# Reads, a short chain and the order of tasks in a fused attention and gated feed-forward layer

## The chip, the cores and the metric

The kernel runs on one core of a Trainium2 chip. The metric is the device time of one execution in microseconds; three runs of the kernel before have a median of 5631.06 us (5629.08 to 5638.95). Beside them there is one profiled execution, on which all readings below rest. Lines (L701) are lines of the kernel before; engines are named TensorE (PE, with its weight loads as PEld), VectorE (DVE), ScalarE (ACT), GpSimd (POOL) and SyncE (SP), which issues all DMAs here.

## What is computed

The input is `x` with 8 batches of 2048 tokens of 512 values. All is float32.

```python
xn = layernorm(x)
q, k, v = xn @ Wq.T + bq, xn @ Wk.T + bk, xn @ Wv.T + bv      # 8 heads: 8 wide for q and k, 64 for v
scores = einsum("bmhd,bnhd->bhmn", q, k) / sqrt(8)
scores = where(scores >= 0, scores, 0.2 * scores)
s = gamma * (softmax(scores) @ v) + xn
base = xn @ W.T
logits = l2norm(xn @ Wp.T + bp) @ l2norm(sim) * exp(min(temp, CLAMP))   # 4 experts
lw = softmax(logits)
ret = where(expert == argmax(lw), lw, 0)
res = sum over experts of ret * (xn @ Wd.T) @ Wu.T            # ranks 1, 2, 4, 8
out = x + s * silu(base + res)
```

## The kernel before

**Tiles and loops.** Tokens are cut into 4 blocks of 512 a batch, heads into 4 pairs. A *sequence step* `s` is one batch, one pair of heads and one block of queries; there are 8 x 16 = 128 of them, and each loops over 16 chunks of 128 keys (`i`). One pass of the inner loop is called a half step: 2048 in all. A half step does, in TensorE's order: the row shift onto the scores of chunk `i` for the first head (`less_max`, L657), the scores of the next chunk (`score`, L640), one unit of the maxima of a later sequence step (`max_unit`, L586), the row shift for the second head, and then either attention weights times values (`weigh`, L681) or a piece of background work. ScalarE makes the leaky slope (L651) and the exp (L669) of both heads; VectorE reduces the unit of maxima from PSUM (L597, into `mxr`); GpSimd adds the exp tile to a running sum (`add_up`, L701, 128 x 1024 float32).

**PSUM.** Scores have two pairs of banks, `mx` of the maxima has one buffer of two banks, `av` one, and all background work and the endings share one bank, `m`.

**Order.** The order of instructions on each engine is written out by hand, by three generators that the loop resumes: `queue[0]` an ending, `queue[1]` the shift rows, `queue[2]` the background tasks. What a generator yields says what may come next: IDLE (resume me once in the next half step, `go_on`), WAIT (nothing else of the background in between), TINY, HOLD, FREE, SLOW (TensorE pieces of several sizes, which `half_full` puts where weights times values would stand, or which `half_light` does in the last batch). `due_at` spreads the tasks' costs over time.

**Shift rows** (`shift_rows`, L597 to L631). At half step 6 of a sequence step the maxima of the next one are complete, and VectorE reduces `mxr` to `m` (L603). In the next half step it takes `big = 0.2 * min(m, 0)` (L609) and `m = max(m, 0)` (L610), and GpSimd does six operations of 128 x 8 (L611 to L616): the sum, and a split into a high and a low part by the factor -4097, into a tile `c`. Both engines work through their queues in order, so these six stand in front of the next L701. Two half steps later VectorE transposes `c` (L621), and eight small DMAs carry the rows through DRAM to `shift`.

**Background tasks.** `project_block` makes queries, keys and values of a block of the next batch (transposes L370 and their copies L373, projections L265 and L279). `lift_block` makes the gate and the feed-forward of a block: in its gate, the logits are multiplied into the bank `gps` (L446), and a chain of some 14 small VectorE operations (L456 to L479) and one exp (L460) turns them, in place in PSUM, to the chosen expert's weight, in three groups with a WAIT between them; copies spread the weight to `rx`. The tasks of a batch are written in the order lift 1, lift 2, project 0, project 1, lift 3, project 2, project 3. `norm` runs the layer norm's statistics of a block ahead of its `project_block`.

**Endings** (`ending`, L703). After the last weights times values of a sequence step: `av` is copied out (L708), three DMAs read rows of the lifted block (`gs` from GS, `xs` from the input and from XN, L714 to L717), after three more half steps TensorE sums `acc` over keys (L724) and transposes (L741), and VectorE divides (L732 to L743), adds XN (L744), multiplies by `gs` (L747) and adds the input (L748). The result goes out from `gs`.

**Start-up.** The first batch's projections and the gate's constants are made ahead of the loop (L863 and on). Two lines of it are spoken of below: L207 multiplies two small SBUF tiles into `simn`, and L222 subtracts two SBUF tiles of 32 x 512 into `wu_sb`; L434, in `lift_block`, is GpSimd's power of four elements a partition.

Of the kernel before, what the change touches and what calls it, by code (L numbers as in the profile page):

```python
# [8 lines left out]
FP = mybir.dt.float32  # L9
# [23 lines left out]
def fused_layer_kernel(  # L33
# [113 lines left out]

    hi_bits = filled("hi_bits", HI_BITS, I32)
    minus_one = filled("minus_one", -1.0)
    splitter = filled("splitter", -4097.0)  # L150
    ln_eps = filled("ln_eps", LN_EPS)

    kst = []
# [144 lines left out]
    def norm(b, n):  # L298
# [24 lines left out]
        normalize(0)  # L323
        normed[b, n] = xn, normalize

    def fetch(b, n):
        xnT = two.tile([128, NC, BLK], FP, name="xnT")
        nc.sync.dma_start(out=xnT, in_=XT[b][n])
        fetched[b, n] = xnT
# [31 lines left out]
    def project_block(b, n, prefetch):  # L361

        for _ in stats.pop((b, n)):
            pass
        xn, normalize = normed.pop((b, n))
        xnT = two.tile([128, NC, BLK], FP, name="xnT")
        for t in range(NT):
            tp = bank([128, NC, 128], "tp")
            for c in range(NC):
                nc.tensor.transpose(tp[:, c, :], xn[:, t, c * 128 : (c + 1) * 128], ident)  # L370
            if t + 1 < NT:
                normalize(t + 1)
            nc.vector.tensor_copy(xnT[:, :, t * 128 : (t + 1) * 128], tp)  # L373
            spend(0.5)
            yield TINY if t + 1 < NT else FREE
        if prefetch:
            fetch(*prefetch)
        nxt = b * NB + n + 2
        if nxt < B * NB:
            load_x(nxt // NB, nxt % NB)  # L380

        ps = bank([128, BLK], "qkps")
        yield from project(ps, wqk_sb, columns(xnT))
        nc.scalar.activation(ps, ps, AF.Identity, bias=bqk_sb)
        yield WAIT
        hi = one.tile([128, BLK], FP, name="hi")
        lo = one.tile([128, BLK], FP, name="lo")
        split_keys(b, n, ps, hi, lo)
        nc.sync.dma_start(out=XN[b][n], in_=xn)
        nc.sync.dma_start(out=XT[b][n], in_=xnT)  # L390
        if n == NB - 1:
            ready.append(b)
        yield FREE

        vb = one.tile([128, NPAIR, NT, 128], FP, name="vb")
        for t in range(NT):
            ps = bank([128, C], "vps")
            yield from token_major(ps, wv_sb, columns(xnT), t)
            add_bias(vb, t, ps)
            yield FREE if prefetch or t + 1 < NT else TINY  # L400
        store_values(b, n, vb)
        if n == NB - 1:
            valued.append(b)

    def lift_block(b, n, prefetch, cols=None):
# [35 lines left out]
        dn = one.tile([128, BLK], FP, name="dn")  # L441
        nc.scalar.copy(dn, ps)
        yield TINY
        gps = bank([128, NT, 2 * NEXP], "gps")
        for t in range(NT):
            nc.tensor.matmul(  # L446
                gps[:, t, 0:NEXP],
                lhsT=pw[:, t * 128 : (t + 1) * 128],
                rhs=simn,
                start=True,  # L450
                stop=True,
            )
        spend(1.0)
        shape = [128, NT, NEXP]
        lg = gps[:, :, 0:NEXP]
        nc.vector.tensor_tensor(lg, lg, nrm.to_broadcast(shape), ALU.mult)  # L456
        red = sm.tile([128, NT, 1], FP, name="red")
        nc.vector.reduce_max(red, lg, axis=AX.X)
        nc.vector.tensor_tensor(lg, lg, red.to_broadcast(shape), ALU.subtract)
        nc.scalar.activation(lg, lg, AF.Exp)  # L460
        yield WAIT
        nc.vector.reduce_sum(red, lg, axis=AX.X)
        nc.vector.reciprocal(red, red)
        nc.vector.tensor_tensor(lg, lg, red.to_broadcast(shape), ALU.mult)

        nc.vector.reduce_max(red, lg, axis=AX.X)
        pick = gps[:, :, NEXP : 2 * NEXP]
        nc.vector.tensor_tensor(pick, lg, red.to_broadcast(shape), ALU.is_equal)
        nc.vector.tensor_tensor(
            pick, pick, prio.unsqueeze(1).to_broadcast(shape), ALU.mult  # L470
        )
        yield WAIT
        nc.vector.reduce_max(red, pick, axis=AX.X)
        own = sm.tile(shape, FP, name="own")
        nc.vector.tensor_tensor(own, pick, red.to_broadcast(shape), ALU.is_equal)
# [123 lines left out]
    def shift_rows(s):  # L599
        if s >= B * SEQ:  # L600
            return
        m = sm.tile([128, 2 * NT, 1], FP, name="m")
        nc.vector.reduce_max(m, mxr.pop(s).rearrange("p e t n -> p (e t) n"), axis=AX.X)  # L603
        yield IDLE

        ml = sm.tile([128, 2 * NT], FP, name="ml")
        c = parts[s % 2][:, 0 : 4 * NT].rearrange("p (i m) -> p i m", i=2)
        big = sm.tile([128, 2 * NT], FP, name="big")
        nc.vector.tensor_scalar(big, m[:, :, 0], 0.0, SLOPE, ALU.min, ALU.mult)  # L609
        nc.vector.tensor_scalar_max(m[:, :, 0], m[:, :, 0], 0.0)  # L610
        nc.gpsimd.tensor_tensor(ml, m[:, :, 0], big, ALU.add)  # L611
        nc.gpsimd.tensor_tensor(big, ml, splitter.to_broadcast([128, 2 * NT]), ALU.mult)
        nc.gpsimd.tensor_tensor(ml, ml, minus_one.to_broadcast([128, 2 * NT]), ALU.mult)
        nc.gpsimd.tensor_tensor(c[:, 1, :], big, ml, ALU.subtract)
        nc.gpsimd.tensor_tensor(c[:, 0, :], big, c[:, 1, :], ALU.subtract)
        nc.gpsimd.tensor_tensor(c[:, 1, :], ml, c[:, 0, :], ALU.subtract)  # L616
        for _ in range(2):
            yield IDLE

        cT = sm.tile([128, 32], FP, name="cT")  # L620
        nc.vector.transpose(cT, parts[s % 2])  # L621
        for q in range(4):
            nc.sync.dma_start(
                out=SH[s % 2][:, :, :, q, :].rearrange("i e t j -> (i e t) j"),
                in_=cT[32 * q : 32 * q + 4 * NT, :],
            )
        shift = qp.tile([128, BLK], FR, name="shift")
        for g in range(4):
            nc.sync.dma_start(
                out=shift[STK * g : STK * g + 2, :].bitcast(FP),  # L630
                in_=SH[s % 2][:, g % 2].rearrange("i t q j -> i (t q j)"),  # L631
            )
        shifts[s] = shift
# [59 lines left out]
    def add_up(s, i, ex):  # L693
# [6 lines left out]
            acc[s] = two.tile([128, 2, BLK], FP, name="acc")  # L700
        nc.gpsimd.tensor_tensor(acc[s], old, ex, ALU.add)  # L701

    def ending(s):  # L703

        b, p, n = where(s)
# [2 lines left out]
        nc.vector.tensor_copy(avs, avt.pop(s))  # L708
        yield IDLE
        sums = acc.pop(s)  # L710
        while (b, n) not in lifted:
            yield IDLE
        gs = two.tile([128, NT, 128], FP, name="gs")
        nc.sync.dma_start(out=gs, in_=GS[b][n][:, :, cols])  # L714
        xs = two.tile([128, 2, NT, 128], FP, name="xs")
        nc.sync.dma_start(out=xs[:, 0], in_=xv[b, n][:, :, cols])
        nc.sync.dma_start(out=xs[:, 1], in_=XN[b][n][:, :, cols])  # L717
        for _ in range(3):
            yield IDLE
        yield TINY  # L720
# [34 lines left out]
    for b in range(B):  # L755
        order = [(lift_block, b, 1, A2), (lift_block, b, 2, A2)]
        if b + 1 < B:
            order += [(project_block, b + 1, 0, A1), (project_block, b + 1, 1, A1), (lift_block, b, 3, A2)]
            order += [(project_block, b + 1, 2, A1), (project_block, b + 1, 3, A1)]
        else:  # L760
            order += [(lift_block, b, 3, A2)]
        total = sum(o[3] for o in order) - (16 * MM if b + 1 < B else 0.0)
        t0, run = SEQ * b + LIFTED, 0.0
        for f, bb, n, cost in order:
            run += cost
            at = min(run / total, 1.0) * ((KEYED if b + 1 < B else LAST) - LIFTED) + t0
            if run > total + 0.01:
                tasks.append((f, bb, n, cost - 16 * MM, at))
                tasks.append((None, bb, n, 16 * MM, SEQ * b + VALUED))
            else:  # L770
                tasks.append((f, bb, n, cost, at))
        if b + 1 < B:
            tasks.append((lift_block, b + 1, 0, A2, SEQ * (b + 1) + LIFTED))
# [7 lines left out]

    def behind():
        jobs = [t for t in tasks if t[0]]
        for k, (f, b, n, _, _) in enumerate(jobs):
            g, bb, nn = (jobs[k + 1] if k + 1 < len(jobs) else (None, 0, 0))[:3]
            if g is project_block:
                stats[bb, nn] = norm(bb, nn)
            if k == 0:
                yield from opening
            else:  # L790
                yield from f(b, n, (bb, nn) if g is lift_block else None)

    back = behind()
    opening = iter(())
    holder = []
    queue = [None, None, back]
    state = [IDLE, IDLE, IDLE]
    due = [0]

    def go(j):  # L800
        state[j] = next(queue[j], None)
# [3 lines left out]

    def ahead():

        return holder or [k for k in (1, 0, 2) if queue[k] is not None and state[k] != IDLE]

    def go_on():  # L810

        for j in range(3):
            if queue[j] is not None and state[j] == IDLE:
                go(j)
        if holder and state[holder[0]] == WAIT:
            go(holder[0])
            return True
# [68 lines left out]
    with tc.manual_schedule():  # L886
# [143 lines left out]
        for s in range(B * SEQ):  # L1030
            for i in range(CH):
                if i <= 3 and s + 2 not in qst and (where(s + 2)[0] in (0, *ready) or i == 3):
                    load_stacks(s + 2)
                if i >= 6 and s + 1 not in vts and (where(s + 1)[0] in valued or i == 13):
                    load_values(s + 1)
                due[0] = due_at(s + (i + 1) / CH)
                u = s * CH + i + CH + LEAD
                nxt = s * CH + i + 1
# [66 lines left out]
```

## Time and profile before

| | us |
|---|---|
| median of three runs | 5631.06 |
| profiled execution | 5619.18 |
| its span | 5617.4 |
| TensorE busy in it | 5378.9 |
| GpSimd busy | 4779.1 |
| ScalarE busy | 4440.7 |
| VectorE busy | 3673.9 |
| mean granted TensorE clock (share of full) | 0.968 |

In the lists of groups a line gives the code line, engine and operation, what is written and read, the shape, the number of instructions, then their busy time and the mean duration of one in ns, then the idle time of the engine just before them and what ended most of it. In a list of waits the three numbers are the sum in us, how often, and the longest. A timeline gives start and length in us, then engine, line and operation; several like instructions in a row are merged (x3). In a table of windows the columns are the stretch, its length, the busy time of TensorE, its weight loads, VectorE, ScalarE and GpSimd (with counts), then the granted TensorE clock, the DMA share and GB/s.

### The profile page before, as it was taken

To read this page: it belongs to the slowest core of one execution; us is meant where nothing else is said; L and a number is where in the kernel's file an instruction comes from. 1 tells how busy PE (TensorE), PEld (TensorE's weight loads), DVE (VectorE), ACT (ScalarE), POOL (GpSimd) and SP (SyncE) were. 2 spreads that over 40 slices of the span, in tenths; PEclk is the share of its full clock that TensorE was granted. 3 is DMA by queue.
4 is the path that set the end of the run, shared out by engine and by line. 5 is a ranking of instruction groups with operands and counts; after the bars stand their busy time and mean duration, and the time that the engine had idled before them with its cause. 6 is when DMAs were issued, how large, how long until landed. Compare 5 with 4: busy or idle time off the path is not lost.

```text
span 5617.4 us, 78032 instructions
## 1 busy us (share of the span) xinstructions
PE 5378.9 (96%) x26258; PEld 1999.1 (36%) x26258; DVE 3673.9 (65%) x4988; ACT 4440.7 (79%) x8627; POOL 4779.1 (85%) x2906
## 2 busy tenths in 40 slices
PE   8999999999999999999999999999999999999998
PEld 3333333333333333333333333333333333333332
DVE  5577666766676666667666666666766766645653
ACT  2788878888888878888788887888878888767777
POOL 1789988888888888888888888888888888878878
PEclk9999999999999999999999999999999999979989
DMA  5333432434324343252432434234343333322221
GB/s 197 106 112 121 128 113 88 128 106 147 104 78 142 93 146 95 76 158 91 142 92 83 147 112 130 80 111 131 107 123 99 102 120 122 100 78 78 71 63 61
DMA packets 528264, 615.38 MB, mean 110 GB/s; under 512 B 44092, under 2 KB 438332, under 8 KB 491768
## 3 DMA queue, kind: packets, MB, share of 16 engines
q1 hardware_dynamic: 527864, 610.39, 35.6%
q8 instruction: 209, 3.42, 0.3%
q14 instruction: 191, 1.56, 0.1%
HBM read 407.88 MB, written 202.38 MB: 109 GB/s over the span
## 4 chain that ended last, share of the span: by engine, by line
PE 80%; ACT 8%; DVE 7%; DMA 2%; issue 2%; SPq 1%; POOL 1%; POOLq 0%; ACTq 0%; DVEq 0%
PE av L681 28%; PE sc L657 16%; PE zps L279 9%; PE vps L279 8%; PE mx L586 7%; ACT ex L669 5%; ACT sc L651 2%; PE pps L265 2%; DVE mxr L597 2%; PE qkps L265 2%; PE dps L265 2%; PE dps L724 1%; DMA xs<-XN 1%; PE atp L741 1%; DVE gs L748 1%
## 5 line engine op out<-in xcount | busy, mean ns | idle before, releaser
L701 POOL TENSOR_TENSOR acc<-acc,ex 128x1024 f32<-128x1024 f32 x1792 | 4231.0, 2361 | 301.7 <-ACT ex L669 189.3
L597 DVE TENSOR_REDUCE mxr<-mx 128x2 f32<-128x1024 f32 x2032 | 2480.2, 1221 | 1260.0 <-PE sc L657 1018.5
L669 ACT ACTIVATE ex<-sc 128x512 f32<-128x512 f32 x4096 | 2231.0, 597 | 972.2 <-PE sc L657 829.0
L651 ACT ACTIVATE sc<-sc 128x512 f32<-128x512 f32 x4096 | 2237.7, 593 | 18.9 <-PE sc L640 18.9
L681 PE MATMUL av<-ex,v_sb 128*64 128x512 f32 x8192 | 2149.5, 630 | 11.6 <-DVE avs L708 9.2
L657 PE MATMUL sc<-shift,ones_r 2*128 2x512 f32 x4096 | 1679.7, 463 | 75.5 <-ACT sc L651 66.9
L586 PE MATMUL mx<-k,q_sb 32*128 32x512 f32 x4096 | 1445.4, 454 | 37.0 <-DVE mxr L597 35.9
L657 PEld LDWEIGHTS sc<-shift,ones_r 2*128 2x128 f32 x4096 | 703.6, 187 | 1560.4 <-ACT sc L651 1450.5
L640 PE MATMUL sc<-q_sb,k 32*128 32x512 f32 x4096 | 1037.4, 503 | 0.0
L681 PEld LDWEIGHTS av<-ex,v_sb 128*64 128x64 f32 x8192 | 469.7, 138 | 839.6 <-issue 805.2
L586 PEld LDWEIGHTS mx<-k,q_sb 32*128 32x128 f32 x4096 | 562.2, 188 | 61.2 <-DVE mxr L597 49.4
L279 PE MATMUL zps<-w_sb,xnT 128*128 128x512 f32 (+1 forms) x1120 | 541.0, 597 | 32.7 <-DMA xnT<-XT 14.1
L279 PE MATMUL vps<-wv_sb,xnT 128*128 128x512 f32 x960 | 475.2, 619 | 7.4 <-DVE gs L748 7.2
L701 POOL TENSOR_TENSOR acc<-ex 128x1024 f32<-128x1024 f32 x128 | 301.8, 2358 | 197.3 <-ACT ex L669 197.3
L640 PEld LDWEIGHTS sc<-q_sb,k 32*128 32x128 f32 x4096 | 385.9, 185 | 0.8 <-issue 0.8
L279 PEld LDWEIGHTS zps<-w_sb,xnT 128*128 128x128 f32 x1120 | 187.6, 192 | 270.3 <-issue 247.9
L279 PEld LDWEIGHTS vps<-wv_sb,xnT 128*128 128x128 f32 x960 | 164.0, 189 | 209.7 <-issue 195.9
L518 DVE SCALAR_TENSOR_TENSOR g<-th,zps 128x512 f32<-128x512 f32 x128 | 88.0, 688 | 189.2 <-ACT th L517 189.2
L611 POOL TENSOR_TENSOR ml<-m,big 128x8 f32<-128x8 f32 x128 | 26.2, 205 | 176.6 <-DVE m L610 176.6
L349 DVE TENSOR_TENSOR vb<-vps,bv_sb 128x512 f32<-128x512 f32 x120 | 83.0, 691 | 95.6 <-PE vps L279 95.4
L265 PE MATMUL dps<-xnT,wd_sb 128*128 128x512 f32 (+1 forms) x280 | 139.1, 607 | 0.0
L265 PE MATMUL pps<-xnT,wp_sb 128*128 128x512 f32 (+1 forms) x280 | 130.9, 585 | 5.0 <-DVE gs L748 5.0
(124 smaller groups left out, 2656.7 us busy)
## 6 DMA issues: line engine op xcount, KB each, us to landing
v_sb<-VS SPq DMA_DIRECT2D x127, 1024.0 KB
k<-KS SPq DMA_DIRECT2D x256, 256.0 KB
XN<-xn SPq DMA_DIRECT2D x32, 1024.0 KB
q_sb<-QS SPq DMA_DIRECT2D x256, 128.0 KB
xnT<-XT SPq DMA_DIRECT2D x32, 1024.0 KB
GS<-g SPq DMA_DIRECT2D x32, 1024.0 KB
gs<-GS SPq DMA_DIRECT2D x128, 256.0 KB
xs<-in_x_dram SPq DMA_DIRECT2D x128, 256.0 KB
```

Source lines behind the costliest of these rows:

```text
L265: nc.tensor.matmul(ps[:, part], lhsT=wt[:, c, :], rhs=xnT[c][:, part], start=(c == 0 and part.start == 0), stop=(c == NC - 1 and part.stop ...
L279: nc.tensor.matmul(ps[:, part], lhsT=xnT[c][:, t * 128 : (t + 1) * 128], rhs=wt[:, c, part], start=(c == 0 and part.start == 0), stop=(c = ...
L349: nc.vector.tensor_tensor(vb[:, :, t, :], ps.rearrange("p (h d) -> p h d", h=NPAIR), bv_sb.rearrange("p (h d) -> p h d", h=NPAIR), ALU.add,)
L518: nc.vector.scalar_tensor_tensor(g[:, t, :], th, 1.0, ps, ALU.add, ALU.mult)
L586: nc.tensor.matmul(parts[e], lhsT=q_sb[r, t * 128 : (t + 1) * 128], rhs=k_sb[r, kb // 2 * BLK : (kb // 2 + 1) * BLK], start=True, stop=True,)
L597: nc.vector.reduce_max(mxr[s][:, :, t, kb : kb + 1], mx, axis=AX.X)
L640: nc.tensor.matmul(sc[e], lhsT=k_sb[r, i // 2 * 128 : (i // 2 + 1) * 128], rhs=q_sb[r, :], start=True, stop=True,)
L651: nc.scalar.activation(sc[e], sc[e], AF.Prelu, alpha=SLOPE)
L657: nc.tensor.matmul(sc[e], lhsT=ones_r[r, :], rhs=shifts[s][r, :], start=False, stop=True, skip_group_check=True,)
L669: nc.scalar.activation(ex[:, e, :], sc[e], AF.Exp, scale=qscale)
L681: nc.tensor.matmul(avt[s][64 * e : 64 * e + DV, :], lhsT=v_sb[:, i, 64 * e : 64 * e + DV], rhs=ex[:, e, :], start=(i == 0), stop=(i == CH ...
L701: nc.gpsimd.tensor_tensor(acc[s], old, ex, ALU.add)
```

## The change

Six edits, together:

- the endings' three reads are issued from the inner loop at chunk 12 and later of their own sequence step, if the block is lifted (`read_for_ending`); the ending itself only reads them where that has not happened;
- the six GpSimd operations and the two VectorE operations of the shift rows become four VectorE `scalar_tensor_tensor`, two in one half step and two in the next, the latter followed at once by the transpose; the loads of `shift` come one half step after it;
- the gate's chain works in the SBUF tiles `lg` and `pick` in place of the bank `gps`, and between its groups it yields TINY and resumes the next `project_block` once (its first two groups of transposes), where the next task is one, and IDLE otherwise;
- tasks alternate: lift 1, project 0, lift 2, project 1, lift 3, project 2, project 3;
- `norm` of a block is begun inside the `project_block` before it;
- a generator that `go_on` has just resumed from IDLE is not taken up a second time in that half step (`been`).

```diff
-        lg = gps[:, :, 0:NEXP]
-        nc.vector.tensor_tensor(lg, lg, nrm.to_broadcast(shape), ALU.mult)
+        lg = sm.tile(shape, FP, name="lg")
+        nc.vector.tensor_tensor(lg, gps, nrm.to_broadcast(shape), ALU.mult)
...
         nc.scalar.activation(lg, lg, AF.Exp)
-        yield WAIT
+        fill, fills[0] = fills[0], None
+        yield TINY if fill else IDLE
+        if fill:
+            next(fill)
...
-        pick = gps[:, :, NEXP : 2 * NEXP]
+        pick = sm.tile(shape, FP, name="pick")
         nc.vector.tensor_tensor(pick, lg, red.to_broadcast(shape), ALU.is_equal)
...
-        yield WAIT
+        yield TINY if fill else IDLE
+        if fill:
+            next(fill)
...
+        m = m[:, :, 0]
         ml = sm.tile([128, 2 * NT], FP, name="ml")
+        big = sm.tile([128, 2 * NT], FP, name="big")
         c = parts[s % 2][:, 0 : 4 * NT].rearrange("p (i m) -> p i m", i=2)
-        big = sm.tile([128, 2 * NT], FP, name="big")
-        nc.vector.tensor_scalar(big, m[:, :, 0], 0.0, SLOPE, ALU.min, ALU.mult)
-        nc.vector.tensor_scalar_max(m[:, :, 0], m[:, :, 0], 0.0)
-        nc.gpsimd.tensor_tensor(ml, m[:, :, 0], big, ALU.add)
-        nc.gpsimd.tensor_tensor(big, ml, splitter.to_broadcast([128, 2 * NT]), ALU.mult)
-        nc.gpsimd.tensor_tensor(ml, ml, minus_one.to_broadcast([128, 2 * NT]), ALU.mult)
-        nc.gpsimd.tensor_tensor(c[:, 1, :], big, ml, ALU.subtract)
-        nc.gpsimd.tensor_tensor(c[:, 0, :], big, c[:, 1, :], ALU.subtract)
-        nc.gpsimd.tensor_tensor(c[:, 1, :], ml, c[:, 0, :], ALU.subtract)
-        for _ in range(2):
-            yield IDLE
+        stt = nc.vector.scalar_tensor_tensor
+        stt(ml, m, SLOPE, m, ALU.mult, ALU.max)
+        stt(big, ml, -4097.0, ml, ALU.mult, ALU.add)
+        yield IDLE
+        stt(c[:, 0, :], ml, -4097.0, big, ALU.mult, ALU.subtract)
+        stt(c[:, 1, :], ml, -1.0, c[:, 0, :], ALU.mult, ALU.subtract)
...
+    def read_for_ending(s):
+        b, p, n = where(s)
+        if s >= B * SEQ or s in reads or (b, n) not in lifted:
+            return
+        cols = slice(p * 128, (p + 1) * 128)
+        gs = two.tile([128, NT, 128], FP, name="gs")
+        nc.sync.dma_start(out=gs, in_=GS[b][n][:, :, cols])
+        xs = two.tile([128, 2, NT, 128], FP, name="xs")
+        nc.sync.dma_start(out=xs[:, 0], in_=xv[b, n][:, :, cols])
+        nc.sync.dma_start(out=xs[:, 1], in_=XN[b][n][:, :, cols])
+        reads[s] = gs, xs
...
-            order += [(project_block, b + 1, 0, A1), (project_block, b + 1, 1, A1), (lift_block, b, 3, A2)]
+            order[1:1] = [(project_block, b + 1, 0, A1)]
+            order += [(project_block, b + 1, 1, A1), (lift_block, b, 3, A2)]
...
-        return holder or [k for k in (1, 0, 2) if queue[k] is not None and state[k] != IDLE]
+        return holder or [k for k in (1, 0, 2) if queue[k] is not None and state[k] != IDLE and k not in been]
...
+                if i >= 12:
+                    read_for_ending(s)
```

More of the change, by code (lines that the diff above doesn't have):

```diff
@@ L149, in fused_layer_kernel @@
     minus_one = filled("minus_one", -1.0)
-    splitter = filled("splitter", -4097.0)
     ln_eps = filled("ln_eps", LN_EPS)
@@ L324, in norm, with begin_norm @@
         normed[b, n] = xn, normalize
+    def begin_norm(k):
+        if k < B * NB:
+            stats[k // NB, k % NB] = norm(k // NB, k % NB)
     def fetch(b, n):
@@ L380, in project_block @@
             load_x(nxt // NB, nxt % NB)
+        begin_norm(nxt - 1)
         ps = bank([128, BLK], "qkps")
@@ L443, in lift_block @@
         yield TINY
-        gps = bank([128, NT, 2 * NEXP], "gps")
+        gps = bank([128, NT, NEXP], "gps")
         for t in range(NT):
             nc.tensor.matmul(
-                gps[:, t, 0:NEXP],
+                gps[:, t, :],
                 lhsT=pw[:, t * 128 : (t + 1) * 128],
@@ L466, in lift_block @@
         nc.vector.reduce_max(red, lg, axis=AX.X)
-        pick = gps[:, :, NEXP : 2 * NEXP]
+        pick = sm.tile(shape, FP, name="pick")
         nc.vector.tensor_tensor(pick, lg, red.to_broadcast(shape), ALU.is_equal)
-        nc.vector.tensor_tensor(
-            pick, pick, prio.unsqueeze(1).to_broadcast(shape), ALU.mult
-        )
-        yield WAIT
+        nc.vector.tensor_tensor(pick, pick, prio.unsqueeze(1).to_broadcast(shape), ALU.mult)
+        yield TINY if fill else IDLE
+        if fill:
+            next(fill)
         nc.vector.reduce_max(red, pick, axis=AX.X)
@@ L626, in shift_rows @@
             )
+        yield IDLE
         shift = qp.tile([128, BLK], FR, name="shift")
@@ L701, in add_up @@
         nc.gpsimd.tensor_tensor(acc[s], old, ex, ALU.add)
+    reads = {}
+    def read_for_ending(s):
[9 more added lines that the diff above has]
+        reads[s] = gs, xs
     def ending(s):
@@ L710, in ending @@
         sums = acc.pop(s)
-        while (b, n) not in lifted:
+        while s not in reads:
+            read_for_ending(s)
             yield IDLE
[L713 to L717, printed above, removed]
+        gs, xs = reads.pop(s)
         for _ in range(3):
@@ L783, in behind @@
         jobs = [t for t in tasks if t[0]]
[L784 to L791, printed above, removed]
+        begin_norm(NB)
+        run = opening
+        for k in range(len(jobs)):
+            nxt = None
+            if k + 1 < len(jobs):
+                f, b, n = jobs[k + 1][:3]
+                g, bb, nn = jobs[k + 2][:3] if k + 2 < len(jobs) else (None, 0, 0)
+                prefetch = (bb, nn) if g is lift_block else None
+                if f is project_block:
+                    nxt = project_block(b, n, prefetch)
+                    fills[0] = nxt if jobs[k][0] is lift_block else None
+                else:
+                    nxt = lift_block(b, n, prefetch)
+            yield from run
+            run = nxt
+    fills = [None]
     back = behind()
@@ L798, in fused_layer_kernel @@
     due = [0]
+    been = []
     def go(j):
@@ L806, in ahead @@
     def ahead():
-        return holder or [k for k in (1, 0, 2) if queue[k] is not None and state[k] != IDLE]
+        return holder or [k for k in (1, 0, 2) if queue[k] is not None and state[k] != IDLE and k not in been]
     def go_on():
-        for j in range(3):
-            if queue[j] is not None and state[j] == IDLE:
-                go(j)
+        been[:] = [j for j in range(3) if queue[j] is not None and state[j] == IDLE]
+        for j in been:
+            go(j)
         if holder and state[holder[0]] == WAIT:
@@ L1035, in fused_layer_kernel @@
                     load_values(s + 1)
+                if i >= 12:
+                    read_for_ending(s)
                 due[0] = due_at(s + (i + 1) / CH)
```

## The prediction

> **What bounds the kernel now.** I read the page first (busy shares, then the costliest groups), then the list of waits of TensorE, then timelines of single half steps.
>
> ```profile
> PE 5378.9 (96%) x26258; PEld 1999.1 (36%) x26258; DVE 3673.9 (65%) x4988; ACT 4440.7 (79%) x8627; POOL 4779.1 (85%) x2906
> L701 POOL TENSOR_TENSOR acc<-acc,ex 128x1024 f32<-128x1024 f32 x1792 | 4231.0, 2361 | 301.7 <-ACT ex L669 189.3
> L597 DVE TENSOR_REDUCE mxr<-mx 128x2 f32<-128x1024 f32 x2032 | 2480.2, 1221 | 1260.0 <-PE sc L657 1018.5
> ```
> TensorE bounds it: 238 us of 5617 are idle. A half step takes 2.67 us (from the first exp at 132 us to the last at 5599, 2047 steps). In it GpSimd adds for 2.36 us and VectorE reduces for 1.22. So GpSimd is nearly always inside an add, and whatever touches the add's port meets one in flight.
>
> ```profile
> PE sc L657 <- ACT sc L651: 66.9, 174, 2.3
> PE mx L586 <- DVE mxr L597: 35.9, 20, 3.7
> DVE atp L744 <- DMA xs<-XN: 25.9, 8, 4.0
> ```
> The second line is how a late VectorE reaches TensorE: the `mx` bank has one buffer, so the next maxima (L586) wait for the reduction L597 before them, and everything behind L586 on TensorE's queue waits too. Eight of these waits follow the third line: an ending whose rows came late.
>
> Now the row that decides this prediction, from the groups with shapes kept apart:
>
> ```profile
> L609 DVE TENSOR_SCALAR big<-m 128x8 f32<-128x8 f32 x128 | 51.3, 401 | 0.0
> L610 DVE TENSOR_SCALAR m<-m 128x8 f32<-128x8 f32 x128 | 22.0, 172 | 4.4
> L611 POOL TENSOR_TENSOR ml<-m,big 128x8 f32<-128x8 f32 x128 | 26.2, 205 | 176.6 <-DVE m L610 176.6
> ```
> Two like instructions, 401 and 172 ns: median L609 is 161, but 22 of 128 take over 1 us. One of them:
>
> ```profile
> 1088.71 7.25 POOL L701 TENSOR_TENSOR acc<-acc,ex 128x1024 f32<-128x1024 f32 x3
> 1094.12 1.87 DVE L609 TENSOR_SCALAR big<-m 128x8 f32<-128x8 f32 x1
> 1098.70 0.50 PE L586 MATMUL mx<-k,q_sb 32*128 32x512 f32 x2 [1.33 <-DVE mxr L597]
> ```
> L609 ends at 1095.99, 0.03 us after the add ends (1088.71+7.25). It stood 1.71 us behind the add, and TensorE lost 1.33 for it two maxima later. The other 106 are quick only because GpSimd's queue holds L611 ahead of the next add, and L611 waits for L610: GpSimd stands there 176.6/127 = 1.4 us a time.
>
> **Part 1, shift rows on VectorE.** Out go L609, L610 and six GpSimd operations (6x0.2 us, plus the 1.4 us of standing); in come four scalar_tensor_tensor, two in one half step and two with the transpose and its DMAs in the next, one half step earlier than before. By the nearest row (L610) they cost 4x0.17, 0.35 us more than the two removed. That would be little. But each reads two SBUF tiles, and nothing holds GpSimd back any more. Does such an operation wait for an add as L609 did? In the steady part no VectorE operation of before reads two SBUF tiles. In the start-up one does:
>
> ```profile
> 111.38 0.20 POOL L614 TENSOR_TENSOR c<-big,ml 128x8 f32<-128x8 f32 x1
> 111.64 1.38 DVE L222 TENSOR_TENSOR wu_sb<-lo,hi 32x512 fp32r<-32x512 f32 x2 [0.68 <-ACT wu_sb L219]
> 111.66 0.73 POOL L615 TENSOR_TENSOR c<-big,c 128x8 f32<-128x8 f32 x1
> ```
> L615, 0.2 us elsewhere, takes 0.73 and ends 0.07 after the first L222: here GpSimd is held by VectorE. Against it stands L207, two SBUF tiles, 0.16 us in the midst of GpSimd's 1.01 us L434 (63.4 us), a power of four elements that may have done its reading. The Trainium skill ("SBUF — State Buffer", section "Who interferes with whom") speaks against the change: a VectorE instruction with two SBUF inputs contends with a GpSimd instruction that reads SBUF, and whichever comes second waits for the whole other one. By the rule an add costs its rest; by L207 nothing. I side with the rule, as L222 is the same kind and L609 shows that the add holds its port to its end.
>
> How long a rest? Taking each L609's start, and letting the add of that half step start when its exp is done and the add before has ended, an add is in flight at 94% of 127 places with 1.73 us to run: mean 1.62. Example: at 2536.15 L609 starts; the exps end at 2535.55, the add before at 2535.82, so the next would run 2535.9 to 2538.26, 2.1 us. VectorE has little room: the ending's L743, L744 (0.7 us each) stand behind these operations, and 1.22+1.4 = 2.62 fills the half step. The 1094 wait of 1.71 cost 1.33, so I take 0.4 as slack: 1.2 us of TensorE per sequence step. The second pair comes with TensorE already stalled and GpSimd drained; I cost no wait, but its 0.6 us now stands ahead of L747, L748: 0.5.
>
> **The stall's tail.** After a stall the matmuls themselves slow, as a wait of 3.08 us at 2071.57 shows:
>
> ```profile
> 2061.00:2068.00 7.00, 7.00 (x49) 2.38 (x45) 4.75 (x8) 6.08 (x12) 6.07 (x3) 1.00 1.09 320
> 2071.50:2077.50 6.00, 5.93 (x18) 1.87 (x18) 2.69 (x7) 1.86 (x4) 5.16 (x8) 0.52 0.16 46
> ```
> The granted clock falls from 1.00 to 0.52, and eight L681 take 3.68 us instead of 1.94: about 2.9 us of the six are lost. The Trainium skill ("TensorE: Matmul & The Clock Gate", section "Why this matters for your kernels") puts the limit at idle gaps over about 3 us; here a gap of 2.3 us (at 1224) did it, and of nine gaps of 1.1 to 1.35 us before L586 four. By the rule stalls of 1.2 us have no tail and 127 of them cost 115 us less; by the rows nearly half have one of about 2 us: 0.9 on average, which I take.
>
> So 1.2+0.5+0.9 = 2.6 us at 127 places, 330. Already paid and gone: the 22 long L609, about 1.6 us each, 35. The second operation of a pair can lose the port again: back-to-back adds lie 78 ns apart, and the first operation fits there, the next hardly. That costs an add more, 2.4, and a tail of 1.5 to 2: 4.4. The bounds are at no place and at all; I take 21 places, 92.
>
> **Part 2, the gate's chain in SBUF.** Same operations, 157 to 182 ns each in PSUM; SBUF saves nothing, since L610 there takes 172. But per block six tensor_tensor now have two SBUF inputs and the four copies to `rx` read SBUF as L609 does, against none before. In three half steps: one waits up to 0.8 us (slack takes it, 0.5 of a stall); the middle group of three loses the port first for about 2.1 us, then for a whole add, 4.5 in all, a stall of 4 with a tail of 1.5; the last group finds GpSimd drained, 1. Together 7 us x 31 blocks (the first runs before the adds) = 217. Bounds: 2 us a block when stalls never come, 15 when both groups lose twice. ScalarE's exp waits for the first group, and its own exps behind it; that is inside the 0.5. The transposes put beside the chain (L370, 74 us in all) are moved, not added; the PSUM bank freed earlier removes part of the 45 us in which TensorE waits for L748: I take 15, bounds 0 and 30.
>
> **Part 3, rows read early.** The three DMAs of an ending are issued at half step 12 of their own sequence step, about ten ahead of use instead of three. No transfer is added, SP's queue gets them ahead of the next stacks' loads, and the blocks are lifted by then (not for five of the 128, four in the last batch). What goes: L744's eight waits for XN, one a batch, worth a stall of 3 to 3.6 us and a tail of about 2.7 each: 8x5.8 = 46. Next late there is VectorE's own chain, which is part 1. Bound: nothing, if another wait takes it.
>
> **Part 4, tasks alternate**, norms begin earlier, and a task just resumed isn't resumed twice: the same instructions, in other half steps. Bounds -20 to +20; I take 0.
>
> **Sum.** Profiled execution 5619.2 (span 5617.4): +330 -35 +92 +217 -15 -46 = 6162. The median of the runs lies 11.9 higher (5631.1): 6174, say 6170.
>
> **The rivals.** *The port is lost at every dependent operation* (adds back to back, each letting one through): 106 more places x 4.4 = 466 and 31 x 6 = 186 on top: about 6820. For it: the 78 ns. Against it: a stalled TensorE soon starves GpSimd. Chance 0.14; own range 6450 to 7000. *Absorbed*: the waits come, but VectorE's 1260 us of idle before L597 take most, no tails: 127x1.0 + 31x2 - 35 - 61 = +93, 5725 (5645 to 5950). Chance 0.15. *No contention*, the side of faster: a two-input operation slips past the add as L207 did, because the add's reading leaves room. Then 35+46+15 fall away: 5535. It decides from a mean wait under the 0.4 us of slack at the first pair. Chance 0.10. Between these two, nothing measurable: 0.02. Likeliest, 6170 (5950 to 6450): 0.59.
>
> The measurement can tell about 0.2%, 11 us, from no change. Faster 0.10, same 0.02, slower 0.88. The range 5660 to 6700 leaves out the no-contention and no-change cases and the upper part of the first rival, about 0.2.
>
> **What would show it.** scalar_tensor_tensor of 128x8 with a mean far over 0.17 us, ends that coincide with the ends of L701; TensorE's wait for mxr grown from 36 us to over 200; granted clock under the 0.968 of before; GpSimd's share down to about 75% with the adds still 2.36 us. If these operations show 0.17 us flat, part 1 and part 2 are wrong and it is faster. If they wait, but TensorE's wait doesn't grow, the slack was larger. If L744's wait for XN stays, part 3 is wrong.

## The result and the profile after

The changed kernel takes 6218.98 us (median of 4 runs, 6211.81 to 6230.19) against 5635.01 us of the kernel before beside it: a ratio of 1.103 (95% interval 1.100 to 1.106). The forecast was slower, with 6170 us as the likeliest time. The profiled execution of the changed kernel has a span of 6219.5 us against 5617.4, so 602 us are to be explained. Line numbers from here on are those of the kernel that is spoken of; in the changed kernel the reduction of the maxima is L604, the maxima L593, weights times values L686, the adds L706, the four shift operations L618, L619, L621 and L622.

The busy shares, from the page of the changed kernel:

```profile
PE 5772.0 (93%) x26258; PEld 2109.0 (34%) x26258; DVE 4027.9 (65%) x5244; ACT 4458.2 (72%) x8627; POOL 4627.2 (74%) x2137
L706 POOL TENSOR_TENSOR acc<-acc,ex 128x1024 f32<-128x1024 f32 x1792 | 4230.6, 2361 | 1134.1 <-ACT ex L674 1086.5
L604 DVE TENSOR_REDUCE mxr<-mx 128x2 f32<-128x1024 f32 x2032 | 2480.0, 1220 | 1440.5 <-PE sc L662 1222.8
```

TensorE has the same 26258 instructions, and yet it is busy for 393 us more; its idle time grew from 238 to 447 us, by 209. The two together are the 602. GpSimd's adds and VectorE's reductions last what they lasted (2.36 and 1.22 us). Neither became slower: both stand idle longer, the reductions for what TensorE makes late, the adds for ScalarE's exps, which wait for TensorE in turn. The waits of TensorE:

```profile
PE mx L593 <- DVE mxr L604: 122.2, 127, 7.0
PE sc L662 <- ACT sc L656: 56.9, 134, 2.2
PE rps L500 <- DVE rx L486: 48.1, 22, 2.4
PE gps L450 <- DVE gs L764: 38.9, 21, 5.7
PE vps L278 <- DVE gs L764: 34.9, 28, 3.2
PE atp L757 <- DVE rd L750: 32.5, 32, 1.9
```

All but the second name VectorE. The wait for `mxr` was 35.9 us in the kernel before. The others are the same lateness seen from another queue place: whatever TensorE asks of VectorE next is late. And VectorE's wait for XN (25.9 us before) is in the list no more. Why VectorE is late stands in the groups with shapes kept apart:

```profile
L618 DVE SCALAR_TENSOR_TENSOR ml<-m 128x8 f32<-128x8 f32 x128 | 193.0, 1508 | 0.2
L619 DVE SCALAR_TENSOR_TENSOR big<-ml 128x8 f32<-128x8 f32 x128 | 71.4, 558 | 4.4
L621 DVE SCALAR_TENSOR_TENSOR c<-ml,big 128x8 f32<-128x8 f32 x128 | 55.0, 430 | 0.0
L622 DVE SCALAR_TENSOR_TENSOR c<-ml,c 128x8 f32<-128x8 f32 x128 | 23.5, 183 | 4.4
L486 DVE COPY rx<-lg 128x128 f32<-128x128 f32 x32 | 41.4, 1294 | 0.0
L471 DVE TENSOR_TENSOR lg<-lg,red 128x16 f32<-128x16 f32 x32 | 28.1, 878 | 1.1
```

Four operations of one shape, with means from 183 to 1508 ns: the shape isn't what costs. At their quickest all four take 0.15 to 0.17 us. Of 127 L618 in the loop 94 take more than 0.4 us, and their ends lie 23 to 28 ns after the end of an add (10th to 90th percentile). One half step in time order, from the timeline of the changed kernel:

```profile
2720.51 2.14 DVE L618 SCALAR_TENSOR_TENSOR ml<-m 128x8 f32<-128x8 f32 x1
2722.69 0.17 DVE L619 SCALAR_TENSOR_TENSOR big<-ml 128x8 f32<-128x8 f32 x1
...
2724.11 1.22 DVE L604 TENSOR_REDUCE mxr<-mx 128x2 f32<-128x1024 f32 x1
2725.24 0.16 DVE L621 SCALAR_TENSOR_TENSOR c<-ml,big 128x8 f32<-128x8 f32 x1
2725.38 0.59 PE L593 MATMUL mx<-k,q_sb 32*128 32x512 f32 x2 [1.63 <-DVE mxr L604]
```

L618 waits 2 us, L619 then slips in, the ending's two operations and the reduction come late, TensorE loses 1.63 us, and L621 finds GpSimd drained. And the clock around it, in windows (the granted clock stands after the five engines' columns, before the DMA share and GB/s):

```profile
2712.00:2720.00 8.00, 8.00 (x50) 2.47 (x46) 5.62 (x9) 6.80 (x15) 7.51 (x4) 1.00 0.01 2
2720.50:2725.30 4.80, 3.25 (x20) 1.13 (x18) 4.73 (x7) 3.05 (x6) 4.49 (x2) 1.00 0.00 0
2725.30:2733.00 7.70, 6.81 (x14) 2.47 (x15) 3.71 (x8) 2.76 (x6) 2.34 (x1) 0.52 0.35 100
```

After 1.63 us of stall the clock stays at about half for the 7.7 us shown, 3.7 us of TensorE's full speed. (The trace's record of the clock has it at half for 10.24 us, from 2725.64 to 2735.88.) Over the execution the granted clock fell from 0.968 to 0.900. Clock missing times span is 0.032 x 5617 = 180 us before and 0.100 x 6219.5 = 622 after: the 442 us more are enough to explain the 393 us of longer busy time.

### The profile page after: what moved, and what is told of

Read it like the earlier page. It is cut to its first block, busy times and chain, and to the rows that moved or that the text cites. A ratio compares the mean times of both kernels' runs of the same rounds, so it can differ in the third digit from the quotient of the medians.

```text
span 6219.5 us, 77594 instructions
## 1 busy us (share of the span) xinstructions
PE 5772.0 (93%) x26258; PEld 2109.0 (34%) x26258; DVE 4027.9 (65%) x5244; ACT 4458.2 (72%) x8627; POOL 4627.2 (74%) x2137
## 4 chain that ended last, share of the span: by engine, by line
PE 73%; DVE 20%; ACT 4%; issue 1%; DMA 1%; POOL 0%; SPq 0%; POOLq 0%; DVEq 0%; ACTq 0%
PE av L686 25%; PE sc L662 13%; PE zps L278 9%; PE vps L278 9%; PE mx L593 7%; DVE mxr L604 6%; DVE ml L618 3%; ACT ex L674 2%; PE pps L264 2%; PE qkps L264 2%; PE dps L264 2%; ACT sc L656 1%; DVE gs L764 1%; PE dps L740 1%; DVE atp L763 1%
## 5 line engine op out<-in xcount | busy, mean ns | idle before, releaser
L706 POOL TENSOR_TENSOR acc<-acc,ex 128x1024 f32<-128x1024 f32 x1792 | 4230.6, 2361 | 1134.1 <-ACT ex L674 1086.5
L604 DVE TENSOR_REDUCE mxr<-mx 128x2 f32<-128x1024 f32 x2032 | 2480.0, 1220 | 1440.5 <-PE sc L662 1222.8
L686 PE MATMUL av<-ex,v_sb 128*64 128x512 f32 x8192 | 2202.3, 643 | 8.5 <-DVE avs L727 4.8
L662 PE MATMUL sc<-shift,ones_r 2*128 2x512 f32 x4096 | 1737.8, 482 | 60.9 <-ACT sc L656 56.9
L593 PE MATMUL mx<-k,q_sb 32*128 32x512 f32 x4096 | 1510.9, 478 | 123.6 <-DVE mxr L604 122.2
L662 PEld LDWEIGHTS sc<-shift,ones_r 2*128 2x128 f32 x4096 | 735.5, 198 | 1641.6 <-ACT sc L656 1354.9
L645 PE MATMUL sc<-q_sb,k 32*128 32x512 f32 x4096 | 1090.6, 528 | 0.0
L686 PEld LDWEIGHTS av<-ex,v_sb 128*64 128x64 f32 x8192 | 474.4, 140 | 866.8 <-issue 841.6
L278 PE MATMUL zps<-w_sb,xnT 128*128 128x512 f32 (+1 forms) x1120 | 653.3, 705 | 35.0 <-DVE gs L764 29.0
L593 PEld LDWEIGHTS mx<-k,q_sb 32*128 32x128 f32 x4096 | 592.5, 198 | 188.9 <-DVE mxr L604 177.6
L278 PE MATMUL vps<-wv_sb,xnT 128*128 128x512 f32 x960 | 551.7, 704 | 35.1 <-DVE gs L764 34.9
L706 POOL TENSOR_TENSOR acc<-ex 128x1024 f32<-128x1024 f32 x128 | 301.9, 2358 | 300.0 <-ACT ex L674 300.0
L278 PEld LDWEIGHTS zps<-w_sb,xnT 128*128 128x128 f32 x1120 | 219.9, 223 | 335.9 <-issue 291.2
L618 DVE SCALAR_TENSOR_TENSOR ml<-m 128x8 f32<-128x8 f32 x128 | 193.0, 1508 | 0.2
L727 DVE COPY avs<-av 128x512 f32<-128x512 f32 x128 | 87.8, 686 | 82.2 <-PE av L686 81.4
```

Source lines behind the costliest of these rows:

```text
L278: nc.tensor.matmul(ps[:, part], lhsT=xnT[c][:, t * 128 : (t + 1) * 128], rhs=wt[:, c, part], start=(c == 0 and part.start == 0), stop=(c = ...
L593: nc.tensor.matmul(parts[e], lhsT=q_sb[r, t * 128 : (t + 1) * 128], rhs=k_sb[r, kb // 2 * BLK : (kb // 2 + 1) * BLK], start=True, stop=True,)
L604: nc.vector.reduce_max(mxr[s][:, :, t, kb : kb + 1], mx, axis=AX.X)
L618: stt(ml, m, SLOPE, m, ALU.mult, ALU.max)
L645: nc.tensor.matmul(sc[e], lhsT=k_sb[r, i // 2 * 128 : (i // 2 + 1) * 128], rhs=q_sb[r, :], start=True, stop=True,)
L662: nc.tensor.matmul(sc[e], lhsT=ones_r[r, :], rhs=shifts[s][r, :], start=False, stop=True, skip_group_check=True,)
```

## The experiments

Theory (port): a VectorE operation that reads two SBUF tiles waits for the GpSimd add in flight; VectorE's lateness stalls TensorE, and each stall is followed by a stretch of lower clock. First rival: the new order of tasks and resumptions costs. Second rival: the chain costs by its place in VectorE's queue, with or without GpSimd.

**One part undone at a time.** The first puts the removed lines of `shift_rows` back into the changed kernel, the second the gate's lines, the third both.

```diff
-        stt(ml, m, SLOPE, m, ALU.mult, ALU.max)
-        stt(big, ml, -4097.0, ml, ALU.mult, ALU.add)
...
+        nc.vector.tensor_scalar(big, m[:, :, 0], 0.0, SLOPE, ALU.min, ALU.mult)
+        nc.vector.tensor_scalar_max(m[:, :, 0], m[:, :, 0], 0.0)
+        nc.gpsimd.tensor_tensor(ml, m[:, :, 0], big, ALU.add)
...
```

> The changed kernel with the shift rows' chain as before (two VectorE operations, six on GpSimd), all else kept. Port theory (a VectorE operation with two SBUF inputs waits for the GpSimd add in flight, VectorE's lateness stalls TensorE at the maxima, and the granted clock falls after the stall): the 255 us of waits of the four shift operations go, and with them about 430 us, to 5790 us (5700 to 5860); granted clock up from 0.90 to about 0.94. Rival, the new order of tasks and resumptions is what costs: within 60 us of the changed kernel's 6219.

Measured: 5792.83 us (5785.34 to 5801.02), clock 0.935. As the port theory had it.

```diff
-        lg = sm.tile(shape, FP, name="lg")
-        nc.vector.tensor_tensor(lg, gps, nrm.to_broadcast(shape), ALU.mult)
+        lg = gps[:, :, 0:NEXP]
+        nc.vector.tensor_tensor(lg, lg, nrm.to_broadcast(shape), ALU.mult)
...
-        yield TINY if fill else IDLE
-        if fill:
-            next(fill)
+        yield WAIT
```

> The changed kernel with the gate's chain as before: in the PSUM bank, with WAIT between its groups, and no transposes of the next block put beside it. Port theory: the 96 us of waits of the gate's operations go, and about 190 us with them: 6030 us (5950 to 6090); the four shift operations still wait. Rival, the order of tasks: 6219 or slower, as the transposes beside the chain are lost.

Measured: 5962.32 us (5956.23 to 5969.69), clock 0.943: 257 us less, more than the 190 expected.

> The changed kernel with both chains as before; what stays of the change is the early reads, the order of tasks, the earlier norms and the single resumption. Port theory: no operation with two SBUF inputs is left in the loop, so it ends a little under the kernel before by the early reads: 5580 us (5530 to 5630). Rival, the order of tasks costs: over 5800.

Measured: 5629.41 us (5614.41 to 5647.11), ratio to before 0.999 (0.998 to 1.000). So taking both chains back gains 590 us, all of the 584 that were lost, and the order of tasks is not the cause of the loss. But the 55 us that I expected below the kernel before aren't there; that is taken up below.

**One part alone.** The kernel before, with only the shift rows' four operations (and the later loads of `shift` that go with them):

> The kernel before with only the shift rows' chain moved to VectorE. Port theory: the scalar_tensor_tensor wait for adds as in the changed kernel, some 250 us of waits, and the time rises by 350 to 450 us: 6035 us (5950 to 6120). Rival, the order of tasks: 5640, as the four operations alone cost 0.17 us each.

Measured: 6020.62 us (6011.70 to 6025.37), 1.067 times before (1.065 to 1.070). TensorE's busy share from its page, and its operations from the groups with shapes kept apart (L611 and L612 are the first pair, L614 begins the second):

```profile
PE 5643.7 (94%) x26258; PEld 2065.3 (34%) x26258; DVE 3964.0 (66%) x5244; ACT 4454.4 (74%) x8627; POOL 4628.6 (77%) x2138
L611 DVE SCALAR_TENSOR_TENSOR ml<-m 128x8 f32<-128x8 f32 x128 | 205.5, 1606 | 0.0
L612 DVE SCALAR_TENSOR_TENSOR big<-ml 128x8 f32<-128x8 f32 x128 | 36.4, 284 | 4.4
L614 DVE SCALAR_TENSOR_TENSOR c<-ml,big 128x8 f32<-128x8 f32 x128 | 102.2, 799 | 0.0
```

And with only the gate's chain in SBUF, its two WAITs kept:

> The kernel before with only the gate's chain moved to SBUF tiles, its WAITs and order kept. Port theory: six operations a block with two SBUF inputs and four copies meet adds in flight, 5 to 8 us a block: 5830 us (5750 to 5900). Rival, the port counts only for the shift rows because the gate's groups have room: within 40 us of 5635.

Measured: 5833.98 us (5819.19 to 5846.35), 1.036 (1.033 to 1.039). In its groups with shapes kept apart the waits are spread otherwise over the chain than in the changed kernel. There the largest copy to `rx` waits longest (mean 1294 ns, against 757 here); here L468, which makes `pick`, and L464, which multiplies by the reciprocal, do:

```profile
L468 DVE TENSOR_TENSOR pick<-lg,red 128x16 f32<-128x16 f32 x32 | 62.4, 1951 | 1.1
L464 DVE TENSOR_TENSOR lg<-lg,red 128x16 f32<-128x16 f32 x32 | 49.9, 1558 | 1.1
L469 DVE TENSOR_TENSOR pick<-pick,prio 128x16 f32<-128x16 f32 x32 | 5.6, 175 | 1.1
L474 DVE TENSOR_TENSOR lg<-lg,own 128x16 f32<-128x16 f32 x32 | 5.6, 175 | 1.1
```

L469 and L474, which follow at once on an operation that has just waited, take 175 ns: the first of two operations waits for an add, and the next comes in before the next add.

**The cause taken away, the operations kept.** Two kernels tell the port from the queue. The first is the changed kernel without three of the fifteen adds of a sequence step; its sums lack three of sixteen terms.

```diff
+        if i in (6, 7, 8):
+            return
         old = acc[s]
```

> The changed kernel with the adds of half steps 6, 7 and 8 of every sequence step left out, so that the sums lack three of sixteen terms; the four shift operations then meet no add in flight. Port theory: all four at 0.16 to 0.17 us flat, and the time falls by the price of part 1, to about 5800 us (5700 to 5900); the gate's operations still wait. Rival, the longer chain on VectorE costs by its own place in the queue and not by waiting for GpSimd: over 6100.

Measured: 5765.04 us (5758.31 to 5773.66). In its groups with shapes kept apart all four are flat:

```profile
L622 DVE SCALAR_TENSOR_TENSOR c<-ml,c 128x8 f32<-128x8 f32 x128 | 21.4, 167 | 4.4
L619 DVE SCALAR_TENSOR_TENSOR big<-ml 128x8 f32<-128x8 f32 x128 | 21.3, 167 | 4.4
L618 DVE SCALAR_TENSOR_TENSOR ml<-m 128x8 f32<-128x8 f32 x128 | 20.0, 156 | 0.2
L621 DVE SCALAR_TENSOR_TENSOR c<-ml,big 128x8 f32<-128x8 f32 x128 | 19.9, 156 | 0.0
```

The same instructions in the same places cost 454 us less when no add is in flight. The gate's waits are as long as ever (98 us, against 96 in the changed kernel), so they have no share in the 454; what it is worth of itself to have 384 adds fewer, this run can't tell. The second keeps all adds and instead makes GpSimd stand, as its own chain did in the kernel before. It is the kernel before with the four operations and, after each pair,

```diff
+        nc.gpsimd.tensor_tensor(idle, ml, big, ALU.add)
...
+        nc.gpsimd.tensor_tensor(idle, ml, c[:, 1, :], ALU.add)
```

> The kernel before with the shift rows' chain on VectorE as in the change, and after each pair of its operations a small GpSimd addition of 128 x 8 that reads their result and whose own result is not used. GpSimd then stands in front of its next add until the pair is done, as it stood at its own chain before. Port theory: the first pair meets an add only where the add before is late (some 25 places), the second meets the last 0.4 us of an add: 80 us of waits in place of 282, and 5700 us (5640 to 5770) in place of 6021. Rival, the four operations cost by their form or their place in VectorE's queue: 6000 or over, as more work is added to GpSimd.

Measured: 5709.11 us (5707.24 to 5711.92), against 6021 without the two additions. More work on GpSimd, 312 us less. Its groups with shapes kept apart show the shelter (L614 is the first addition), and what is left of the waits:

```profile
L614 POOL TENSOR_TENSOR idle<-ml,big 128x8 f32<-128x8 f32 x128 | 26.3, 206 | 176.2 <-DVE big L612 151.9 <-ACT sc L652 23.4 <-ACT ex L670 0.9
L611 DVE SCALAR_TENSOR_TENSOR ml<-m 128x8 f32<-128x8 f32 x128 | 53.5, 418 | 0.0
L616 DVE SCALAR_TENSOR_TENSOR c<-ml,big 128x8 f32<-128x8 f32 x128 | 46.2, 361 | 0.0
```

GpSimd stands for 176 us in front of the first addition, as long as at its chain in the kernel before (176.6), and the time is shorter with this standing than without it.

**The early reads, and a chain that needs no port.** The kernel before with only the reads:

> The kernel before with only the endings' reads issued early. Theory: the eight waits of VectorE for XN (25.9 us) go, with a stall of 3 to 3.6 us and a slow stretch of about 2.7 each: 5590 us (5580 to 5605). Rival, another wait takes their place: 5625 to 5640.

Measured: 5580.51 us (5569.27 to 5637.78), ratio 0.992 (0.989 to 0.996). The reads alone gain 56 us by the medians; but the runs fall in two groups, six from 5569 to 5583 and two at 5636 and 5638, where nothing is gained. The profiled execution is one of the six; why the other two gain nothing stays open. TensorE's wait for `mxr`, from its list of waits, falls from 35.9 us with 3.7 as the longest to

```profile
PE mx L586 <- DVE mxr L597: 11.4, 10, 1.4
```

So the kernel with both chains back has lost this gain elsewhere. The tensor_scalar that waited in the kernel before is the likely place, here with both chains back and then with the reads alone:

```profile
L614 DVE TENSOR_SCALAR big<-m 128x8 f32<-128x8 f32 x128 | 65.2, 510 | 0.2
L609 DVE TENSOR_SCALAR big<-m 128x8 f32<-128x8 f32 x128 | 47.2, 369 | 0.0
```

With both chains back it waits at 33 places, 46 us in all, and TensorE's wait for `mxr` is 38.1 us; with the reads alone it waits at 20 places, 26 us. At 1.6 to 1.9 us of span for each us of such waits (worked out at the end) the 20 us more are 32 to 38 of the missing 49, an estimate. To take this operation away, ScalarE makes the leaky maximum in the kernel with both chains back:

```diff
-        nc.vector.tensor_scalar(big, m[:, :, 0], 0.0, SLOPE, ALU.min, ALU.mult)
-        nc.vector.tensor_scalar_max(m[:, :, 0], m[:, :, 0], 0.0)
-        nc.gpsimd.tensor_tensor(ml, m[:, :, 0], big, ALU.add)
+        nc.scalar.activation(ml, m[:, :, 0], AF.Prelu, alpha=SLOPE)
```

> The changed kernel with the gate's chain as before and the shift rows' chain as before but for its first step: ScalarE makes the leaky maximum in one operation in place of VectorE's two and GpSimd's first. Then no operation of VectorE in the loop needs the port, since the tensor_scalar that waited for adds at 22 places is gone as well. Port theory: 20 to 40 us under the kernel with both chains back, about 5550 us. Rival: the small operation on ScalarE holds up its exps, and nothing is gained.

Measured: 5554.34 us (5541.76 to 5567.64), ratio 0.986 (0.984 to 0.989): the fastest of all kernels here, 75 us under the one with both chains back, about twice the 20 to 40 expected. The same step in the kernel before, alone and then with the early reads:

> The kernel before with only the leaky maximum made by ScalarE. Port theory: its 30 us of waits of the tensor_scalar go, and 30 x 1.75 = 50 us with them: 5585 us (5570 to 5600). Rival, that VectorE's waits at 22 places were hidden: 5635.

Measured: 5597.54 us (5585.31 to 5604.93), ratio 0.993 (0.992 to 0.995). The waits of the kernel before weren't hidden, though they were worth 37 us and not 50. (They are 31 us at 23 places where L609 takes over 0.4 us; at 18 of them it takes over 1 us.)

> The kernel before with two edits: the endings' reads issued early, and the leaky maximum made by ScalarE in one operation, so that no VectorE operation in the loop needs the port; order of tasks, gate and resumptions as before. Over the kernels run so far the span rises by about 1.75 us for each us that VectorE waits for the port (0 us of waits at 5558, 354 at 6220). Port theory: the 26 us of waits that the early reads alone still had go, 45 us under that kernel's 5581: 5535 us (5520 to 5555), and no slower than the kernel with the new order of tasks and ScalarE's step (5554). Rival, the new order of tasks is worth something of its own: over 5560.

Measured: 5565.94 us (5541.16 to 5573.74), ratio 0.987 (0.985 to 0.990). This misses the range expected, 5520 to 5555, and lies where the rival had it, over 5560: the two gains are 56 and 37 alone and 68 together, though no operation of VectorE waits for an add any more. In this execution TensorE is idle for 187 us, less than in the fastest kernel (196), but at a lower clock (0.964 against 0.970); two sequence steps of 49 and 51 us, at places that take 40 to 43 in the other batches, are part of it. With the tensor_scalar gone the two orders of tasks are 12 us apart, where they were 49 apart with it. Whether the new order is worth these 12 of itself stays open: the runs of the two kernels overlap.

## Why the prediction was right, and where its terms were off

**The rule against the row.** Taking the port's rule over L207, which showed no wait, was the choice that decided, and it held: with the adds away the operations are flat. L222 was the right nearest row. Why L207 didn't wait beside L434 stays open. The no-contention case, 5535, is somewhat below the kernels in which nothing of VectorE waits for an add (5554 and 5566).

**Part 1** was forecast at 387 us net (330 + 92 - 35). Undone in the changed kernel, it is worth 426; alone in the kernel before, 388; with the adds away, 454. The terms: 94% of places at 1.73 us were reckoned, and 74% (94 of 127) waited, 1.5 us mean duration over all (alone in the order of before, 110 of 127 and 1.6 us). 21 second losses were taken, and L619 has 24; as the 21 was picked between no place and all, that is luck. For the second pair no wait was costed, and L621 has 18, 30 us in all. The reading "22 of 128 take over 1 us" was too high: 18 do, and 23 take over 0.4. The 35 us that were subtracted for them agree with the 37 measured.

**Part 2** was forecast at 217 - 15. Undone, it is worth 257; alone, 197. Within it the groups were distributed wrongly. I took two lost adds for the middle group; the operations behind the first wait mostly slip in, and the group lost 39 us instead of some 140. I took the last group as drained; it lost 50, most of it in the largest copy to `rx`, and TensorE waits for that copy directly (48 us, L500).

**The two parts together.** In the kernel with both chains back, the gate's chain alone adds 163 us (5629 to 5793), the shift rows' alone 333 (to 5962), both 590: 93 more than the sum. The prediction added them up. The excess isn't in TensorE's idle time, which the chains lengthen by 48 and 188 us alone and by 221 together, but in its busy time, by 129 and 151 alone and by 376 together. So it is the lower clock that makes the two worse together than apart. In 18 of 32 blocks the gate's first group stands right behind the second pair, so that stalls of both fall close to each other; that this is the reason isn't shown.

**The tail was mis-sized, and the stalls hid it.** In the sum, before what was subtracted, about 435 us were stalls and 200 tails. Measured are, net, 209 us of added idle time and 393 of slower matmuls. The step that failed is "by the rows nearly half have one of about 2 us: 0.9 on average". The share was about right and the size was wrong. The kernel with the four operations alone shows it: its record of the clock has 97 stretches at half clock against 41 before, so 56 more, which is nearly half of 127. But it has 891 us of them against 361, so that the added ones last 9.5 us on average and take 4.7 us of full speed each, where the prediction took about 2. Its matmuls are slower by 265 us (5643.7 against 5378.9), 2.1 a place where 0.9 was taken (1.2 with the tails of the 21 second losses). Its idle time rose by 141 us (380 against 238), 1.1 a place where 1.7 was taken (1.2 and 0.5; 2.1 with the second losses). In the changed kernel it is the same: 129 stretches at half clock, 1250 us, 9.7 us each; and 354 us of port waits made only 209 us of idle time, net of what the early reads removed. Two errors of opposite sign, stalls too long and tails too short, cancelled: that the total came so near is in this part luck. That TensorE's wait for `mxr` would pass 200 us was wrong as well: it is 122, with the rest of TensorE's waits for VectorE under other names.

**Part 3** was forecast at 46 and measured 56 alone; its sign that L744's wait goes was right. **Part 4** was taken at 0. With both chains back the reads' gain is not seen: the old tensor_scalar meets more adds in the new order, and with it gone the two orders are within 12 us. **GpSimd's share** came to 74% (75 forecast).

## What to carry to other kernels

Before a small operation is moved to VectorE, count its SBUF inputs and look at what GpSimd runs at that moment: with adds in flight nearly always, 0.17 us became 1.5. A tensor_scalar or a copy with one SBUF input can wait too (L609 before, the copies to `rx`). Over these kernels each microsecond of such waits cost 1.6 to 1.9 of the span ((6220-5558)/354 is 1.9, (6024-5617)/(282-30) is 1.6). An engine that stands can be a shelter: while GpSimd stood in front of its six small operations, no add of it was in flight for VectorE to wait for, and to take them away was to lose that. ScalarE does the leaky maximum without the wait (5554 us), and with the operand in PSUM the gate's operations didn't wait (157 to 182 ns each).

## What was not expected of the hardware

TensorE's clock fell after much shorter gaps than I had taken, and than the rule that the prediction weighed against its rows would have it. In the changed kernel 71 of 72 gaps of 1.5 to 2 us are followed within 5 us by slow matmuls (128x512 over 0.85 us), and 35 of 41 from 1.1 to 1.5; before, it was 4 of 10 from 1.1 to 1.5. By the record of the clock three of the 72 begin at half clock already; of the other 69, 68 are followed by a fall within 3.5 us, and before 23 of these falls there is no other gap over 0.3 us in the last 6.8 us.

The idle time summed over a step of the clock tells about the same. In these traces the clock is granted in full or at half, and but for the last stretch of the execution each stretch at half lasts a whole multiple of 3.41 us. If the time at full clock in the changed kernel is cut into such steps, of those with more than 1.5 us of TensorE idle 77 of 78 are followed by half clock; with less than 0.8 us, 2 of 1221; in between, 43 of 94. In the kernel before it is 21 of 23 over 1.5 us, 8 of 1451 under 0.8, and 7 of 28 in between. Counted with its tail, a us of added idle time cost about 2.9 us of span (602 for 209; with the four operations alone, 406 for 141).

A copy in SBUF of 128x128 waits for an add as a tensor_scalar does (mean 1294 ns against 280 from PSUM), ending 0.06 to 0.09 us after the add. And the second of two dependent operations usually gets in before the next add, although adds that follow at once begin 78 ns after the last one: L619 lost its place in 24 of 127.
